# Low digits of x by ScalarE and an accumulating DMA, and causal masks of three units moved from TensorE to VectorE, in a fused attention and FFN kernel

## The chip, the cores and the metric

The kernel runs on one core of one Trainium2 chip. The metric is the device time of one execution in microseconds. Three runs of the kernel before gave 1025.21, 1024.13 and 1023.95 us, median 1024.13. The profiled execution took 1023.99 us.

A core has five engines, each with its own queue: TensorE (PE in the profile; its weight loads are PEld), VectorE (DVE), ScalarE (ACT), GpSimd (POOL) and SyncE (SP, which here only issues transfers). Each runs its own instructions in order and waits on semaphores of the others. Transfers (DMA) run beside them, issued here from SP's, ScalarE's and POOL's queues.

## The reference

One transformer block over x of 4 sequences x 512 positions x 1024 channels, in fp32:

```
q, k, v = x @ wq.T, x @ wk.T, x @ wv.T        # 16 heads of 64
q, k    = rope(q), rope(k)                    # pairs (x1, x2) -> (-x2, x1)
scores  = where(causal, q @ k.T, -1e9) / 8
a       = softmax(scores) @ v
x       = layernorm(x + a @ wo.T)
x       = layernorm(x + x @ (w8 * scales).T)  # w8 is int8
```

## The kernel before

**Digits.** A matmul with fp32 operands costs more on TensorE than one with the rounded type fp32r. So each fp32 operand is split: h is the operand times LESS = 1 - 2^-13, rounded to fp32r; l = x - h is the rest; d = h - l / X12 with X12 = 2^-12. A product is 16 matmuls of h with h and l with l, interleaved (the A part), and 8 of d with d (the D part), over 8 blocks of 128 channels; the two parts are combined with factors 1 + X12 and -X12. For x, h comes from ScalarE (`high_x`, L169), l from VectorE (`low_x`, L173), d from VectorE (`diff_x`, L177). Each of these instructions handles one of four chunks n of 2 x 512 columns per partition (512 KB in fp32). Weights are split likewise (L214, L215, L219, L223).

**Units.** There are 32 units, each a sequence b and a pair of heads: units 0 to 15 alternate between b = 0 and 1, units 16 to 31 between b = 2 and 3. The digits of two sequences are kept at a time: `XD[0]` for even b and `XD[1]` for odd. So around units 14 to 17 the digits of b = 2 and 3 replace those of 0 and 1. Near the end "b = 4" and "b = 5" stand for the two halves of the output weights wo, which take the places of the digits of x in the same way. `new_sequence` (L324) writes down when that is done, `load_x2` (L165) loads a chunk into one of three staging buffers (pool `stage`, which also holds staged weights, tiles of ao and rows of x).

**One unit's loop.** TensorE computes the scores of unit u (L409), and in between, as 72 "tickets", the products q, k, v of the coming units: (u+1, k), (u+1, v), (u+2, q). VectorE takes the maxima (L430), ScalarE the exponentials (L444), VectorE the reciprocals (L452), POOL the scaling (L458), VectorE the 32 x 32 transposes (L463); SP takes the probabilities through DRAM (`turned`, L464, then `prT`, L472) to finish the transposition. The values of a unit are turned in the same manner (`turn_values`: L464, then four transfers `va`, L482). TensorE then multiplies probabilities by values (`attend`, L490); ScalarE copies the result out (`ot`, L498) and issues its transfer to ao in DRAM (L499). The A part of a product is taken from PSUM by ScalarE (`tA`, L295), the D part by VectorE, which adds tA (L318). A and D tiles share a pool of two PSUM buffers (`pj`). For q and k SP swaps neighbouring rows (`rot<-raw`, two transfers, L249), and VectorE does the three rope steps (L235, L236, L242).

**Causal mask.** In the units listed in BUSY (L136) TensorE adds the mask to the diagonal blocks itself: eight matmuls of `unit` with `mask` in bfloat16 per unit (L419). In the other units VectorE adds it, four instructions per unit (L427).

**Order of work.** The order on TensorE, VectorE and ScalarE is that of the program text. Work for coming units is put into named slots of a loop with `later(u, slot, f)` and done there with `run(u, slot)`. The slots stand in this order: early, (maxima, exponentials of score groups 0 and 1), between, 18 tickets, (exponentials of group 2, attend u-1), after, first transposes, more tickets, first, turn, mid, tickets, second, tickets, late, tickets, values of u+1, tickets, end. The orders of SP and POOL are worked out by a scheduler from the dependences.

**The end.** Loops 30 and 31 also compute the first output products (`out_product`, L199) with the digits of wo; rows of x for the residual are loaded to the staging buffers or to the tables of cos and sin (`more_rows`, `rows_of_tables`), and VectorE adds the product to a row (L208). Then the int8 words of the FFN are loaded and cast (L620), and for each of 16 row tiles the output product, the norm, the transposition and the FFN product (`ffn`, L672) follow each other; POOL issues the transfers of the result (L685).

Of the kernel before, what the change touches and what calls it, by code (L numbers as in the profile page):

```python
# [38 lines left out]
def attention_ffn_kernel(  # L39
# [93 lines left out]
    units = [(b, hp) for hp in range(NHP) for b in (0, 1)] + [(b, hp) for hp in range(NHP)[::-1] for b in (2, 3)]  # L133
    NU = len(units)

    BUSY = (0, 1, NU // 2 - 2, NU // 2 - 1, NU - 2, NU - 1)  # L136
    qk, prod, va, plan = {}, {}, {}, {}


# [10 lines left out]
    def later(u, slot, f):  # L150
        plan.setdefault((u, slot), []).append(f)
# [19 lines left out]
    def low_x(b, n):  # L171
        h, l, d = (t[:, 2 * n : 2 * n + 2, :] for t in XD[b % 2])
        nc.vector.tensor_tensor(l, staged.pop((b, n)), h, SUB)  # L173

    def diff_x(b, n):
        h, l, d = (t[:, 2 * n : 2 * n + 2, :] for t in XD[b % 2])
# [52 lines left out]
    with tc.tile_pool(name="raw", bufs=2) as rawp, tc.tile_pool(name="qk", bufs=2) as qkp, ExitStack() as heads:  # L229
# [38 lines left out]
        def product(u, k, n):  # L268

            b, hp = units[u]  # L270
            w, r = WD[k], XD[b % 2]
            if n in (0, 2 * NC):
                prod["A" if n == 0 else "D"] = pjp.tile([P, S], FP, tag="pj", name=f"p_{u}_{k}_{n}")
            ps = prod["A" if n < 2 * NC else "D"]
            c, part = (n // 2, n % 2) if n < 2 * NC else (n - 2 * NC, 2)
            nc.tensor.matmul(  # L276
                ps,
                lhsT=w[part][:, c, :],
                rhs=r[part][:, c, :],
                start=n in (0, 2 * NC),  # L280
                stop=n in (2 * NC - 1, NT - 1),
            )
            last = u == NU - 1
            more = last or units[u + 1][1] != hp

            if more and n == 0:
                load_ao(k) if last else load_w(k, units[u + 1][1])

            b_next = units[u + 2][0] if u + 2 < NU else B + b % 2
            x_next = k == 2 and b_next != b  # L290
            if x_next and n == 0:
                new_sequence(u, b_next, True)
            if n == 2 * NC - 1:
                prod["tA"] = rawp.tile([P, S], FP, tag="tA", name=f"tA_{u}_{k}")
                nc.scalar.activation(prod["tA"], ps, AF.Copy, scale=1.0 + X12)  # L295
                if x_next:
                    new_sequence(u, b_next, False)
                if more:

                    scalar = ("after" if last else None, "first", None)[k]  # L300
                    if scalar:
                        later(u - 1, scalar, lambda: high_w(k))
                    else:
                        high_w(k)
                    vector = ((u - 1, "first"), (u - 1, "late"), (u, "between"))[k]
                    if u == 1:
                        vector = (None, vector, (1, "between"))[k]
                    if last and k != 1:
                        l, d = (((u - 1, "turn"), (u - 1, "mid")), None, ((u, "after"), (u, "after")))[k]
                        later(*l, lambda: low_w(k))  # L310
                        if k == 2:

                            later(*l, lambda: low_x(b_next, 0))
                        later(*d, lambda: diff_w(k))
                    else:
                        later(*vector, lambda: split_w(k))
            if n == NT - 1:
                nc.vector.scalar_tensor_tensor(raw_tile(u, k), ps, -X12, prod["tA"], op0=MUL, op1=ADD)  # L318
                if k < 2:
                    swap(u, k)  # L320
                    slot = ("first" if last else "between" if u % 2 else "late") if k == 0 else "turn"
                    later(u - 1, slot, lambda: rope(u, k))

        def new_sequence(u, b, begin):  # L324


            if b == B + 1:
                if begin:
                    later(u - 1, "mid", lambda: load_x2(b, 0))
            else:  # L330
                for n in range(3):
                    (load_x2 if begin else high_x)(b, n)
            if begin:
                return

            def each(f, *ns):
                return lambda: [f(b, n) for n in ns]

            if b <= B:
                steps = (  # L340
                    (u - 1, "late", each(low_x, 0)), (u - 1, "late", each(load_x2, 3)),
                    (u - 1, "late", each(low_x, 1, 2)), (u - 1, "end", each(high_x, 3)),
                    (u, "between", each(low_x, 3)), (u, "between", each(diff_x, 0, 1)),
                    (u, "late" if b == B else "first", each(diff_x, 2, 3)),
                )
            else:

                steps = (
                    (u - 1, "late", each(load_x2, 1)), (u - 1, "late", each(high_x, 0)),
                    (u - 1, "late", lambda: load_x2(b, 2, qkp.tile([P, 2, S], FP, tag="qk", name="last_2"))),  # L350
                    (u, "early", lambda: load_x2(b, 3, qkp.tile([P, 2, S], FP, tag="qk", name="last_3"))),
                    (u, "after", each(high_x, 1, 2)), (u, "first", lambda: more_rows(2)),
                    (u, "first", each(high_x, 3)), (u, "first", each(low_x, 1, 2)),
                    (u, "second", each(low_x, 3)), (u, "second", lambda: more_rows(3)),
                    (u, "late", each(diff_x, 0, 1, 2, 3)),
                )
            for step in steps:
                later(*step)

        def more_rows(t):  # L360
            row_tiles.append(stage(f"row_{t}", [P, E]))
            load_row(t)
# [140 lines left out]
        with tc.manual_schedule(  # L503
            engines={mybir.EngineType.PE, mybir.EngineType.DVE, mybir.EngineType.Activation}
        ):
            with tc.tile_pool(name="first", bufs=1) as firstp:
                raw_w = firstp.tile([P, 3, NC, P], FP, name="raw_w")
                raw_x0 = firstp.tile([P, NC, S], FP, name="raw_x")
                last_x1 = firstp.tile([P, 2, S], FP, name="last_x1")
                for c in range(0, NC, 2):  # L510
                    nc.sync.dma_start(out=raw_w[:, 0, c : c + 2, :], in_=wq[0, :, c : c + 2, :])
                    nc.scalar.dma_start(out=raw_x0[:, c, :], in_=xT[0, :, c, :])
                    nc.sync.dma_start(out=raw_x0[:, c + 1, :], in_=xT[0, :, c + 1, :])
                nc.sync.dma_start(out=raw_w[:, 1], in_=wk[0])
                load_x2(1, 0)
                nc.sync.dma_start(out=raw_w[:, 2], in_=wv[0])
                load_x2(1, 1)
                nc.sync.dma_start(out=cos_sb, in_=cos)
                nc.sync.dma_start(out=sin_sb, in_=sin)
                load_x2(1, 2)  # L520
                staged[1, 3] = last_x1
                nc.sync.dma_start(out=last_x1, in_=xT[1, :, 6:8, :])
                for n in range(NC // 2):
                    staged[0, n] = raw_x0[:, 2 * n : 2 * n + 2, :]
                raw_x = [[staged[b, n] for n in range(NC // 2)] for b in range(2)]


                def first_high_w(k):
                    nc.scalar.activation(WD[k][0], raw_w[:, k], AF.Copy, scale=LESS)

                def first_low_w(k):
                    nc.vector.tensor_tensor(raw_w[:, k], raw_w[:, k], WD[k][0], SUB)
                    nc.scalar.activation(WD[k][1], raw_w[:, k], AF.Copy, scale=1.0 / X12)

                for n in range(NC // 2):
                    high_x(0, n)
                    low_x(0, n)
                for n in range(3):
                    diff_x(0, n)
                whole_product(0, 0)  # L540
                first_high_w(1)
                for n in range(2):
                    high_x(1, n)
                    low_x(1, n)
                rope(0, 0)
                whole_product(0, 1)
                for n in range(2, 4):
                    high_x(1, n)
                    low_x(1, n)
                first_high_w(2)  # L550
                first_low_w(1)
                rope(0, 1)
                whole_product(0, 2)
                for n in range(2):
                    diff_x(1, n)
                first_low_w(2)
                for n in range(2, 4):
                    diff_x(1, n)
                diff_w(1)
                whole_product(1, 0)  # L560
                load_w(0, 1)
# [10 lines left out]
            for u in range(NU):  # L572
# [6 lines left out]
                run(u, "between")  # L579
                take(18)  # L580
                softmax(u, 2)
                if u:
                    attend(u - 1)
                run(u, "after")
# [183 lines left out]
```

## Time and profile before

| | |
|---|---|
| median of three runs | 1024.13 us |
| profiled execution | 1023.99 us |
| its span | 1022.2 us |
| TensorE busy | 1004.3 us, 98% |
| VectorE busy | 849.0 us, 83% |
| ScalarE busy | 388.9 us, 38% |
| POOL busy | 202.4 us, 20% |
| scores of unit 14 begin | 335.14 us |
| scores of unit 15 begin | 359.79 us |
| scores of unit 16 begin | 382.64 us |
| scores of a plain unit after the one before (77.85 to 99.30) | 21.45 us |

The span is from the first to the last instruction in the trace; the time of an execution is 1.8 us longer here. Matmuls overlap: 128x512 matmuls that follow each other without a pause start 0.227 us apart, although each lasts 0.39. The granted clock is that of TensorE, 1.00 when full. In a line of the timeline the columns are start, duration, engine, line of the kernel, operation, output and inputs, and in brackets the idle time of the engine before it with what ended it. In a line of the waits the columns are the waiting instruction, what it waited for, the total in us, how many times, and the longest. In a group's line the columns are the line, engine, operation and tiles, the count, the busy time in us and the mean of one in ns, and the idle time before. In a line of the transfers the columns are the tiles, the queue, the count, the size of one, and the median time in us from issue to landing.

### The profile page before, as it was taken

Reading aid. Unit: us, or ns where it says so; the run is one execution under the profiler, and the core shown is the slowest. Engines: PE = TensorE matmul, PEld = TensorE weight load, DVE = VectorE, ACT = ScalarE, POOL = GpSimd, SP = SyncE. Lnnn points to the kernel's source line nnn. Section 1 sums busy time; section 2 is a strip of 40 time slices with the busy share of each in tenths; the row PEclk is TensorE's granted clock in tenths of the full one; section 3 lists DMA queues with packets and bytes.
Section 4 is the critical chain, followed back from the end, with each engine's and each line's share of the span. In section 5 each row is a group of like instructions: output and inputs, shape, how many; then the busy total and the mean of one; then the engine's idle time right before and its main releaser. Section 6 shows DMA issues by size and latency. Waiting matters only on the chain.

```text
span 1022.2 us, 13786 instructions
## 1 busy us (share of the span) xinstructions
PE 1004.3 (98%) x4652; PEld 745.7 (73%) x4652; DVE 849.0 (83%) x1234; ACT 388.9 (38%) x841; POOL 202.4 (20%) x283
## 2 busy tenths in 40 slices
PE   9999999999999999999999999998899999999997
PEld 4667777777777677777777777776588888888885
DVE  5988888888888889888888888888898877878776
ACT  4524444354544434445344443444442122121110
POOL 0122232222322322332223322222200000000000
PEclk9999999999999999999999999999899999999998
DMA  7576676766768777676776768678645465553641
GB/s 287 168 232 218 203 230 189 264 214 212 216 201 265 240 250 235 188 247 199 246 219 202 236 195 257 216 239 272 221 130 156 126 160 139 133 166 103 144 104 62
DMA packets 264022, 204.09 MB, mean 200 GB/s; under 512 B 147600, under 2 KB 220304, under 8 KB 263824
## 3 DMA queue, kind: packets, MB, share of 16 engines
q1 hardware_dynamic: 256464, 185.64, 60.8%
q10 hardware_dynamic: 5328, 9.70, 2.6%
q0 software_dynamic: 2160, 7.87, 1.9%
q8 instruction: 37, 0.61, 0.2%
q14 instruction: 33, 0.27, 0.1%
HBM read 112.46 MB, written 73.92 MB: 182 GB/s over the span
## 4 chain that ended last, share of the span: by engine, by line
PE 86%; DMA 5%; DVE 5%; ACT 1%; issue 1%; SPq 0%; POOL 0%; DVEq 0%; ACTq 0%; POOLq 0%
PE p L276 43%; PE y L199 16%; PE f L672 11%; PE s L409 6%; PE o L490 6%; PE pw L261 2%; ACT pr L444 1%; DMA turned<-pr 1%; DMA sx<-in_wo 1%; DMA sx<-in_xT 1%; DVE pr L463 1%; DVE x_l L173 1%; DMA cos_sb<-in_x 1%; DMA raw_x<-in_xT 1%; POOL pr L458 0%
## 5 line engine op out<-in xcount | busy, mean ns | idle before, releaser
L458 POOL TENSOR_SCALAR pr<-pr,rden 128x128 f32<-128x128 f32 (+3 forms) x256 | 191.5, 770 | 531.3 <-DVE rden L452 369.0
L276 PE MATMUL p<-x_h,w_h 128*128 128x512 f32 x736 | 290.1, 394 | 0.0
L276 PE MATMUL p<-x_l,w_l 128*128 128x512 f32 x736 | 286.8, 390 | 0.0
L276 PE MATMUL p<-x_d,w_d 128*128 128x512 f32 x736 | 190.8, 395 | 1.2 <-DVE v L318 1.0
L276 PEld LDWEIGHTS p<-x_h,w_h 128*128 128x128 f32 x736 | 138.1, 188 | 48.1 <-issue 19.7
L444 ACT ACTIVATE pr<-s,nmx 128x128 f32<-128x128 f32 (+3 forms) x256 | 131.4, 530 | 100.0 <-DVE nmx L430 100.0
L276 PEld LDWEIGHTS p<-x_d,w_d 128*128 128x128 f32 x736 | 135.6, 188 | 34.1 <-issue 5.1
L276 PEld LDWEIGHTS p<-x_l,w_l 128*128 128x128 f32 x736 | 138.2, 188 | 28.1
L295 ACT ACTIVATE tA<-p 128x512 f32<-128x512 f32 x92 | 55.1, 599 | 219.8 <-PE p L276 219.7
L463 DVE STREAM_TRANSPOSE pr<-pr 128x768 f32<-128x768 f32 (+1 forms) x96 | 99.5, 1054 | 22.2 <-POOL pr L458 21.0
L199 PE MATMUL y<-x_h,w_h 128*128 128x512 f32 x256 | 102.9, 402 | 4.5 <-DVE row L208 3.8
L199 PE MATMUL y<-x_l,w_l 128*128 128x512 f32 x256 | 102.3, 400 | 1.9 <-DVE w_l L219 1.9
L430 DVE TENSOR_REDUCE nmx<-s 128x2 f32<-128x256 f32 (+3 forms) x128 | 101.3, 819 | 2.9 <-PE s L419 0.2
L672 PE MATMUL f<-wf,x1lo 128*128 128x512 f32 x240 | 93.5, 390 | 0.0
L672 PE MATMUL f<-wf,x1hi 128*128 128x512 f32 x240 | 93.5, 389 | 0.0
L409 PE MATMUL s<-qk 64*128 64x384 f32 (+3 forms) x512 | 82.6, 450 | 1.0 <-DVE qk L242 1.0
L490 PE MATMUL o<-prT,va 128*64 128x256 f32 (+3 forms) x512 | 76.0, 439 | 0.0
L223 DVE TENSOR_TENSOR w_d<-w_h,w_l 128x1024 fp32r<-128x1024 f32 x60 | 74.4, 1240 | 1.5
L318 DVE SCALAR_TENSOR_TENSOR raw<-p,tA 128x512 f32<-128x512 f32 x61 | 41.9, 687 | 38.2 <-PE p L276 38.1
L490 PEld LDWEIGHTS o<-prT,va 128*64 128x64 f32 x512 | 33.9, 136 | 45.6 <-issue 40.3
L199 PE MATMUL y<-x_d,w_d 128*128 128x512 f32 x256 | 63.7, 390 | 0.0
L199 PEld LDWEIGHTS y<-x_h,w_h 128*128 128x128 f32 x256 | 49.6, 194 | 16.0 <-DVE row L208 4.3
(112 smaller groups left out, 1157.0 us busy)
## 6 DMA issues: line engine op xcount, KB each, us to landing
turned<-pr SPq DMA_DIRECT2D x64, 384.0 KB, 3.3
rot<-raw SPq DMA_DIRECT2D x128, 128.0 KB, 2.4
turned<-pr SPq DMA_DIRECT2D x32, 512.0 KB, 4.5
prT<-turned SPq DMA_DIRECT2D x32, 512.0 KB, 5.0
prT<-turned SPq DMA_DIRECT2D x32, 384.0 KB, 4.2
turned_v<-v SPq DMA_DIRECT2D x32, 256.0 KB, 4.6
va<-turned_v SPq DMA_DIRECT2D x128, 64.0 KB, 2.6
prT<-turned SPq DMA_DIRECT2D x32, 256.0 KB, 3.3
```

The source lines that it names most:

```text
L199: nc.tensor.matmul(ps, lhsT=r[part][:, c, :], rhs=w[part][:, c, :], start=n in (0, 2 * NC), stop=n in (2 * NC - 1, NT - 1),)
L223: nc.vector.tensor_tensor(d, h, l, SUB)
L276: nc.tensor.matmul(ps, lhsT=w[part][:, c, :], rhs=r[part][:, c, :], start=n in (0, 2 * NC), stop=n in (2 * NC - 1, NT - 1),)
L295: nc.scalar.activation(prod["tA"], ps, AF.Copy, scale=1.0 + X12)
L318: nc.vector.scalar_tensor_tensor(raw_tile(u, k), ps, -X12, prod["tA"], op0=MUL, op1=ADD)
L409: nc.tensor.matmul(ps[:, j, at : at + n], lhsT=t[rows, 0, ts(i, P)], rhs=keys[rows, :, : (i + 1) * Q], start=True, stop=u not in BUSY,)
L430: nc.vector.tensor_reduce(nmx[:, 2 * i : 2 * i + 2], ps[:, :, at : at + n], AX.X, ALU.max, negate=True)
L444: nc.scalar.activation(pr[:, :, at // P : at // P + i + 1, j, :], ps[:, j, at : at + n].rearrange("p (r k s) -> p r k s", r=R, s=Q), AF.Ex ...
L458: nc.gpsimd.tensor_scalar(p, p, rden[:, m : m + 1], 1.0, ALU.mult, ALU.mult)
L463: nc.vector.transpose(t, t)
L490: nc.tensor.matmul(ps[j * D : (j + 1) * D, kb * P :], lhsT=v[:, kb, 2 * j : 2 * j + 2, :].rearrange("p a s -> p (a s)"), rhs=t[:, :, 4 * k ...
L672: nc.tensor.matmul(ps, lhsT=part[:, c, :], rhs=wfv[:, c, o], start=(c == 0 and part is hi), stop=(c == NC - 1 and part is lo),)
```

## The change

- BUSY holds three units instead of six: 0, 30 and 31. Units 1, 14 and 15 lose their mask matmuls (24 in all), and VectorE adds the mask there (12 instructions in all).
- A new `digits_x` makes h and l of a chunk. ScalarE makes h as before, then writes -LESS times the staged chunk, rounded to fp32r, into l; this is -h. Then a transfer from POOL's queue adds the staged chunk onto l in SBUF. It replaces the pair of ScalarE's h and VectorE's l for every chunk but the four of b = 0: 20 of 24.
- The places change. For b = 2, 3 and 4, chunks 0 to 2 are done where only h was made before (in the product (u, v), after the A part); the load of chunk 3 moves from slot late to slot end of loop u-1, and its digits to slot between of loop u. For b = 5, chunk 0 is done in (30, late), chunks 1 and 2 in a new slot "then" (after the exponentials of group 2), chunk 3 in slot first; the loads of two rows of x move to slot second. At the start the digits of b = 1 are made in the same places by the new function.

The diff:

```diff
-    BUSY = (0, 1, NU // 2 - 2, NU // 2 - 1, NU - 2, NU - 1)
+    BUSY = (0, NU - 2, NU - 1)
...
+    def digits_x(b, n):
+
+        h, l, d = (t[:, 2 * n : 2 * n + 2, :] for t in XD[b % 2])
+        high_x(b, n)
+        nc.scalar.activation(l, staged[b, n], AF.Copy, scale=-LESS)
+        nc.gpsimd.dma_start(out=l.bitcast(FP), in_=staged.pop((b, n)), accum_op=ADD)
...
                         later(*l, lambda: low_w(k))
-                        if k == 2:
-
-                            later(*l, lambda: low_x(b_next, 0))
                         later(*d, lambda: diff_w(k))
...
                 for n in range(3):
-                    (load_x2 if begin else high_x)(b, n)
+                    (load_x2 if begin else digits_x)(b, n)
...
             if b <= B:
                 steps = (
-                    (u - 1, "late", each(low_x, 0)), (u - 1, "late", each(load_x2, 3)),
-                    (u - 1, "late", each(low_x, 1, 2)), (u - 1, "end", each(high_x, 3)),
-                    (u, "between", each(low_x, 3)), (u, "between", each(diff_x, 0, 1)),
+                    (u - 1, "end", each(load_x2, 3)), (u, "between", each(digits_x, 3)),
+                    (u, "between", each(diff_x, 0, 1)),
                     (u, "late" if b == B else "first", each(diff_x, 2, 3)),
                 )
             else:
 
                 steps = (
-                    (u - 1, "late", each(load_x2, 1)), (u - 1, "late", each(high_x, 0)),
+                    (u - 1, "late", each(load_x2, 1)), (u - 1, "late", each(digits_x, 0)),
                     (u - 1, "late", lambda: load_x2(b, 2, qkp.tile([P, 2, S], FP, tag="qk", name="last_2"))),
                     (u, "early", lambda: load_x2(b, 3, qkp.tile([P, 2, S], FP, tag="qk", name="last_3"))),
-                    (u, "after", each(high_x, 1, 2)), (u, "first", lambda: more_rows(2)),
-                    (u, "first", each(high_x, 3)), (u, "first", each(low_x, 1, 2)),
-                    (u, "second", each(low_x, 3)), (u, "second", lambda: more_rows(3)),
+                    (u, "then", each(digits_x, 1, 2)), (u, "first", each(digits_x, 3)),
+                    (u, "second", lambda: (more_rows(2), more_rows(3))),
                     (u, "late", each(diff_x, 0, 1, 2, 3)),
                 )
...
                 for n in range(2):
-                    high_x(1, n)
-                    low_x(1, n)
+                    digits_x(1, n)
                 rope(0, 0)
                 whole_product(0, 1)
                 for n in range(2, 4):
-                    high_x(1, n)
-                    low_x(1, n)
+                    digits_x(1, n)
...
                 softmax(u, 2)
+                run(u, "then")
                 if u:
                     attend(u - 1)
```

## The prediction

> **What bounds the kernel now.** I read the page's busy shares first, then TensorE's waits, then the places of the longest waits in its timeline, then the granted clock there.
>
> ```profile
> PE 1004.3 (98%) x4652; PEld 745.7 (73%) x4652; DVE 849.0 (83%) x1234; ACT 388.9 (38%) x841; POOL 202.4 (20%) x283
> PE 86%; DMA 5%; DVE 5%; ACT 1%; issue 1%; SPq 0%; POOL 0%; DVEq 0%; ACTq 0%; POOLq 0%
> ```
>
> TensorE is busy 98% of the span and carries 86% of the chain that ended last. Time can only come from matmuls taken off TensorE, from its waits, or from its clock. VectorE has 17% free over the whole span. All of TensorE's waits:
>
> ```profile
> PE y L199 <- DVE row L208: 3.8, 1, 3.8
> PE y L199 <- DVE w_l L219: 1.9, 1, 1.9
> PE s L409 <- DVE qk L242: 1.0, 1, 1.0
> PE p L276 <- DVE v L318: 1.0, 1, 1.0
> PE y L199 <- DVE cos_sb L208: 0.6, 1, 0.6
> PE p L276 <- DVE raw L318: 0.2, 1, 0.2
> ```
>
> Apart from 1.5 us at the first memset and 0.2 for a load, TensorE waits 8.7 us in all, always for VectorE, in six places. The timeline shows where (the bracket is the idle time before):
>
> ```profile
> 350.94 2.11 PE L276 MATMUL p<-x_d,w_d 128*128 128x512 f32 x8 [0.21 <-DVE raw L318]
> 357.72 2.14 PE L276 MATMUL p<-x_d,w_d 128*128 128x512 f32 x8 [1.03 <-DVE v L318]
> 702.38 0.50 PE L199 MATMUL y<-x_l,w_l 128*128 128x512 f32 x1 [1.93 <-DVE w_l L219]
> 731.83 0.80 PE L199 MATMUL y<-x_h,w_h 128*128 128x512 f32 x1 [3.85 <-DVE row L208]
> ```
>
> Two lie in the loop of unit 14, where the digits change from batches 0 and 1 to 2 and 3; the others lie at the start (55.01, 1.04) and in loops 30 and 31. The windows view (columns: stretch, length, busy time of PE, PEld, DVE, ACT, POOL, granted clock, DMA share, GB/s) gives the clock:
>
> ```profile
> 350.90:359.80 8.90, 7.83 (x34) 5.86 (x34) 8.87 (x10) 3.90 (x5) 0.00 (x1) 1.00 0.83 265
> 703.00:706.40 3.40, 3.40 (x10) 2.63 (x9) 3.37 (x5) 0.00 (x0) 0.00 (x0) 0.50 1.02 357
> 730.30:737.10 6.80, 5.27 (x12) 4.14 (x13) 6.70 (x7) 0.00 (x0) 0.00 (x0) 0.50 0.91 273
> ```
>
> After the wait of 1.03 the clock stayed full. After 1.93 came 3.40 us at half, in which 10 matmuls ran at about 0.43 us each instead of 0.227; that costs 1.7. So a wait of some 2 us is charged almost twice.
>
> **The change part by part.** VectorE loses 20 subtractions and gains 12 mask additions; ScalarE gains 20 copies, POOL 20 transfers:
>
> ```profile
> L173 DVE TENSOR_TENSOR x_l<-sx,x_h 128x1024 fp32r<-128x1024 f32 x17 | 20.4, 1232 | 0.0
> L427 DVE TENSOR_TENSOR s<-s,mask 128x256 f32<-128x256 f32 x104 | 44.5, 427 | 3.6
> L169 ACT ACTIVATE x_h<-sx 128x1024 fp32r<-128x1024 f32 x17 | 17.3, 1054 | 25.1 <-DMA sx<-in_wo 13.0 <-DMA sx<-in_xT 11.7 <-ACT ot L498 0.4
> ```
>
> VectorE: 20 x 1.22 - 12 x 0.43 = 19.3 us less. ScalarE: 20 x 1.05 = 21 us more. Neither sum counts by itself; what counts is six places on TensorE. Against them stands that the low digit is now ready only when a transfer has landed, and that the staging buffer, of which there are three, is free only then. No row shows an accumulating transfer. The nearest:
>
> ```profile
> out<-row POOLq DMA_DIRECT2D x7, 512.0 KB, 4.0
> row<-in_x SPq DMA_DIRECT2D x8, 512.0 KB, 3.7
> sx<-in_xT SPq DMA_DIRECT2D x11, 512.0 KB, 5.5
> turned_v<-v SPq DMA_DIRECT2D x32, 256.0 KB, 4.6
> ```
>
> I bound the time L from issue to landing by 3.7 (the quickest 512 KB) and 9 (the table load at the start, 9.0), and take 5: POOL's own row of 4.0, raised because 512 KB takes 5.5 in the attention part.
>
> The Trainium skill, "DMA: Bandwidth & Descriptors", section "Anatomy of one DMA — SWDGE (gpsimd) path", fits 2.0 us plus bytes over 436 GB/s, an estimate of 3.2 us for 512 KB. POOL's row of 4.0 is longer already; by the page the forecast would be nearer to the faster rival.
>
> *Start.* Unit 1's eight mask matmuls leave TensorE. Scores with masks last 55.01 to 58.71, 3.70; those of a plain unit 77.85 to 80.21, 2.36. That is -1.34. The wait of 1.04 before them stays: VectorE's chain there hangs on unit 0's last exponentials, which stand on ScalarE behind the copy tA that TensorE releases (41.31). The low digits of batch 1 issue near 25 and are wanted near 38 by VectorE's queue, so 9 us is hidden. Bounds -2.4 (the wait goes too) and 0 (four additions, 1.7 us, delay unit 1's softmax as much). Taken: -1.34.
>
> *Loop of unit 14.* Masks -1.34; the two waits, 1.24, could go. The D product of (16,0) would then start at 357.72 - 1.34 - 1.24 = 355.1. But it needs the buffer that the evacuation of v_15 empties, behind rope (15,1) on VectorE. On SP the load of chunk 2 of batch 3 waits until the accumulation of chunk 3 of batch 2 has landed, and the turned probabilities and the swap of raw (15,1) are queued behind it. POOL issues that accumulation between the scalings of groups 1 and 2, near 346.0. Then: + L + 0.5 (load issue) + 0.5 (turned issue) + 0.6 (first half of the swap) + 2.4 (landing) + 2.05 (three rope steps) + 0.65 (evacuation) = 352.7 + L = 357.7. TensorE waits 2.6, and D starts as before: net 0.0. The clock: 2.6 is nearer to 1.93 than to 1.03, so +1.7. Taken: +1.7. Bounds: L = 3.7 gives 356.4, a wait of 1.3, no drop: -1.3; L = 9 gives 361.7: +4.0 + 1.7 = +5.7.
>
> *Loop of unit 15.* Masks -1.34. The load of chunk 3 of batch 3 was issued at 358.83, before the values were turned; now it stands on SP behind turned_v of unit 15 and its four va loads:
>
> ```profile
> 358.83 0.34 SPq L165 DMA_DIRECT2D sx<-in_xT  x1
> 361.72 0.33 SPq L464 DMA_DIRECT2D turned_v<-v  x1
> 365.04 2.58 SPq L482 DMA_DIRECT2D va<-turned_v  x4
> ```
>
> Count from E, the end of v_15's evacuation. Turned_v issues at E+0.8, lands at +5.4 (4.6), the va issues end at +8.0, a swap is between them, the load issues at +8.6, lands at +13.0 (4.4 as now), then h and l on ScalarE (2 x 1.05) and the copy tA of (16,1) (0.6): +15.7. TensorE wants that PSUM buffer for A of (16,2) at E+12.2, by the present timeline without masks. Wait 3.5, then 3.4 us at half clock, +1.7: -1.34 + 3.5 + 1.7 = +3.9. Bounds: turned_v landing in 3.3, as in this very unit, and the load in 3.7 give a wait of 1.5, below 1.93, no drop: +0.2; a load of 5.5 gives +5.0.
>
> The Trainium skill, "TensorE: Matmul & The Clock Gate", section "Why this matters for your kernels", asks for no idle gaps over about 3 us, since a whole idle window of 3.4 us halves the clock. The row at 702.38 speaks against it: 1.93 us was followed by a window at 0.50. By the rule the wait of 2.6 would keep the clock, and the sum would be 1.7 lower.
>
> *End.* Three low digits of wo's second half (1.18 + 2.34 us at 727.73) leave VectorE ahead of row L208, so the wait of 3.85 goes, and perhaps the half clock behind it (2.6). But the A product then needs digits whose transfers POOL issues after all scalings of unit 31 (717.82 + 7.08 = 724.9) and which land near 731; the differences (4.62) follow, and o of unit 31 starts at 736 at best instead of 739.99: -4.0. Not all reaches the end: the copy ot of unit 31 stands on ScalarE behind digits of a tile of ao that SP loads late (13.89 us of waiting at 738.54), and its transfer releases the int8 words, their casts and the first FFN product, which started without slack at 759.83. That caps the gain near 2. Behind the transfer of chunk 3 of wo's first half SP now holds a load of ao and the swap of raw (31,1): +0.7. Taken: -1.3. Bounds -4.2 and +2.5 (L = 9 makes that swap 4 later, less 1.5 of slack). The wait of 1.93 is for w_l and stays. POOL's 20 issues of 0.53 (its row for out) cost 10.6 us on an engine that is 80% idle: nothing, with the 80% as cover.
>
> Sum: -1.34 + 1.7 + 3.9 - 1.3 = +3.0 on the profiled execution's 1023.99, which is 0.14 below the median 1024.13: 1027.0.
>
> **The rivals.** *Faster.* Transfers land in 3.7 and the values in 3.3, no wait reaches 1.9, the clock stays: -1.34 - 1.3 + 0.2 - 3.0 = -5.4, about 1018.5. For it: POOL's 4.0, and the 3.3 seen in unit 15. Against it: the DMA engines are 0.75 and 0.81 busy in those two loops.
> *Same.* The new waits come, but without the half clock: 3.0 - 3.4 = -0.4, 1023.6.
> *Much slower.* L near 9, because three accumulations run together beside other transfers; it decides from L = 6.5, where unit 14's loop loses 1.5 more. All upper ends: -1.34 + 5.7 + 5.0 + 2.5 = +11.9, 1036.
> *It does not do what it says:* VectorE never was the limit, so only the 24 mask matmuls count: -4.0, 1020. TensorE's waits for it, 8.7 us, speak against.
>
> **How the numbers follow.** A measurement tells 0.2% (2.05 us) from no change: faster is below 1022.1, slower above 1026.2. Forecast 0.40 (1024.5 to 1030), faster rivals 0.28 together, same 0.18, much slower 0.14. A fifth of the forecast's own range lies below 1026.2: same 0.26, slower 0.46. The range 1018.0 to 1032.5 leaves out some 0.09 on either side.
>
> **What would show it.** In the changed profile: a wait of A of (16,2) for ScalarE's tA of about 3.5; a wait of D of (16,0) for v of about 2.6; clock 0.50 in windows between 355 and 380; the first A product of wo's second half no longer waiting for VectorE's row; the wait of 1.04 at unit 1 unchanged; landing of x_l from POOL's queue near 5. Wrong if the va loads do not hold back that load, or if ScalarE takes tA earlier.

## The result and the profile after

The changed kernel took 1054.62 us (median of 4 runs, 1053.96 to 1056.07), the kernel before beside it 1024.49; the ratio is 1.0303, 95% interval 1.0290 to 1.0316. It is slower by 3%, and outside the range of the prediction. The profiled execution has a span of 1053.0 us, 30.8 more than before.

Two lines of the page of the kernel after, busy times and the chain that ended last:

```profile
PE 1012.7 (96%) x4628; PEld 751.9 (71%) x4628; DVE 832.1 (79%) x1226; ACT 407.1 (39%) x861; POOL 215.2 (20%) x303
PE 83%; DMA 8%; DVE 5%; ACT 1%; issue 1%; SPq 1%; DVEq 0%; POOL 0%; ACTq 0%
```

VectorE did get lighter, by 16.9 us (19.3 forecast). But transfers now hold 8% of the chain, where it was 5%, and TensorE 83% in place of 86%. TensorE was given 24 matmuls less and yet is busy 8.4 us longer, since it ran at half clock more often (the granted clock is in the windows below). All waits of TensorE of 1 us and more, in the view of the waits of the kernel after:

```profile
PE p L283 <- ACT tA L302: 12.0, 3, 4.9
PE y L206 <- DMA x_l<-sx: 3.8, 1, 3.8
PE y L206 <- DVE v L322: 3.5, 1, 3.5
PE p L283 <- DVE v L322: 3.3, 1, 3.3
PE y L206 <- DMA x_l<-last: 3.2, 2, 1.8
PE o L492 <- DMA prT<-turned: 2.1, 1, 2.1
PE warm L81 <- DVE sin_sb L79: 1.5, 1, 1.5
PE f L673 <- DVE x1lo L647: 1.1, 1, 1.1
PE s L411 <- DVE qk L249: 1.0, 1, 1.0
```

The waits of 3.85 for VectorE's row and of 1.93 for w_l are gone, as the change would have it. In their place are three waits for ScalarE's tA, two for the evacuation of v, three for low digits themselves and one for turned probabilities. Each of these nine ends, when followed back, at a transfer: ScalarE stands before tA because a load (`sx`) is late, the evacuation of v stands behind a swap that is late. The table compares the two kernels by stretches between the first scores of units (in us, from the timelines; the scores of unit 16 begin at 382.57 before, not 382.64):

| stretch | before | after | difference |
|---|---|---|---|
| start to scores of unit 1 | 55.01 | 54.88 | -0.13 |
| loop of unit 1 | 22.77 | 22.05 | -0.72 |
| units 2 to 13 | 257.36 | 257.36 | 0.00 |
| loop of unit 14 | 24.65 | 32.17 | +7.52 |
| loop of unit 15 | 22.78 | 31.10 | +8.32 |
| units 16 to 29 | 300.25 | 300.25 | 0.00 |
| loop of unit 30 | 26.61 | 35.84 | +9.23 |
| scores of unit 31 to the first FFN product | 50.24 | 55.44 | +5.20 |
| from there to the end | 262.53 | 263.91 | +1.38 |

All but 1.38 us of what was lost was lost where digits are made (the 1.38 go with waits of 0.77 and 1.07 for the digits of the first FFN product). The windows view over the four long stretches (length, busy times, granted clock, DMA share, GB/s), first the kernel before, then the kernel after:

```profile
335.14:359.79 24.65, 23.41 (x114) 15.88 (x113) 21.88 (x28) 10.26 (x24) 8.06 (x8) 1.00 0.75 240
359.79:382.57 22.78, 22.78 (x114) 16.04 (x113) 20.35 (x28) 8.60 (x23) 7.08 (x8) 1.00 0.82 257
682.82:709.43 26.61, 24.68 (x113) 17.10 (x112) 23.02 (x31) 13.79 (x27) 7.09 (x8) 0.94 0.84 259
709.43:759.67 50.24, 45.75 (x210) 33.22 (x209) 42.74 (x57) 20.75 (x37) 8.31 (x9) 0.93 0.63 207
```

```profile
334.29:366.46 32.17, 25.24 (x105) 17.72 (x104) 19.01 (x28) 13.95 (x28) 10.04 (x13) 0.88 0.98 252
366.46:397.56 31.10, 25.58 (x106) 18.55 (x105) 18.84 (x28) 9.42 (x24) 7.14 (x9) 0.85 0.87 260
697.81:733.65 35.84, 27.44 (x113) 18.35 (x112) 20.30 (x27) 16.00 (x29) 8.18 (x11) 0.86 0.93 266
733.65:789.09 55.44, 47.61 (x209) 33.82 (x208) 37.58 (x50) 22.30 (x38) 9.64 (x12) 0.87 0.76 215
```

The DMA engines are 0.98 busy in the loop of unit 14 instead of 0.75, and move hardly more bytes per second (252 GB/s, 240 before). The clock falls to 0.85 to 0.88. In the loop of unit 14, TensorE waits 3.66 and 3.27, 6.9 us, and the clock of 0.88 is worth 0.12 x 32.17 = 3.9; less the masks (1.34) and the old waits (1.24) that makes 8.2, near the 7.5 seen. An estimate, since clock and waits are added as if they were apart.

### The profile page after: what moved, and what is told of

Its sections match the earlier page's. It is cut to its first block, busy times and chain, and to the rows that moved or that the text cites. A ratio compares the mean times of both kernels' runs of the same rounds, so it can differ in the third digit from the quotient of the medians.

```text
span 1053.0 us, 13822 instructions
## 1 busy us (share of the span) xinstructions
PE 1012.7 (96%) x4628; PEld 751.9 (71%) x4628; DVE 832.1 (79%) x1226; ACT 407.1 (39%) x861; POOL 215.2 (20%) x303
## 4 chain that ended last, share of the span: by engine, by line
PE 83%; DMA 8%; DVE 5%; ACT 1%; issue 1%; SPq 1%; DVEq 0%; POOL 0%; ACTq 0%
PE p L283 44%; PE y L206 13%; PE f L673 11%; PE s L411 6%; PE o L492 6%; DMA turned_v<-v 3%; PE pw L268 3%; DMA turned<-pr 2%; DMA rot<-raw 1%; DVE pr L465 1%; DMA cos_sb<-in_x 1%; DMA sc<-in_scales 0%; DMA raw_ao<-ao 0%; SPq L484 0%; DVE nmx L432 0%
## 5 line engine op out<-in xcount | busy, mean ns | idle before, releaser
L283 PE MATMUL p<-x_h,w_h 128*128 128x512 f32 x736 | 294.9, 401 | 12.0 <-ACT tA L302 12.0
L283 PE MATMUL p<-x_l,w_l 128*128 128x512 f32 x736 | 290.6, 395 | 0.0
L460 POOL TENSOR_SCALAR pr<-pr,rden 128x128 f32<-128x128 f32 (+3 forms) x256 | 187.0, 749 | 472.3 <-DVE rden L454 321.9
L283 PEld LDWEIGHTS p<-x_h,w_h 128*128 128x128 f32 x736 | 140.7, 191 | 64.5 <-issue 22.0
L283 PEld LDWEIGHTS p<-x_l,w_l 128*128 128x128 f32 x736 | 140.7, 191 | 28.9
L206 PE MATMUL y<-x_d,w_d 128*128 128x512 f32 x256 | 66.5, 403 | 3.5 <-DVE v L322 3.5
L242 DVE TENSOR_TENSOR rot<-rot,sin_sb 128x512 f32<-128x512 f32 x64 | 44.1, 688 | 30.7 <-DMA rot<-raw 30.7
```

Of the source, the lines that this page charges most:

```text
L206: nc.tensor.matmul(ps, lhsT=r[part][:, c, :], rhs=w[part][:, c, :], start=n in (0, 2 * NC), stop=n in (2 * NC - 1, NT - 1),)
L242: nc.vector.tensor_mul(rot, rot, sin_sb[:, k, :])
L283: nc.tensor.matmul(ps, lhsT=w[part][:, c, :], rhs=r[part][:, c, :], start=n in (0, 2 * NC), stop=n in (2 * NC - 1, NT - 1),)
L460: nc.gpsimd.tensor_scalar(p, p, rden[:, m : m + 1], 1.0, ALU.mult, ALU.mult)
```

## The experiments

Two theories were set against each other. **A**: the transfers cost; an adding transfer from SBUF to SBUF is dear for the DMA engines, lands late, and makes others late. **B**: the places cost; the load of chunk 3 now stands behind the turned values on SP, and its digits stand ahead of tA on ScalarE.

**VectorE adds instead of the transfer** (the change without its transfer: all new places, loads, masks and ScalarE copies).

```diff
-        nc.gpsimd.dma_start(out=l.bitcast(FP), in_=staged.pop((b, n)), accum_op=ADD)
...
+    def add_x(b, n):    # called in the slots where low_x stood before
+        l = XD[b % 2][1][:, 2 * n : 2 * n + 2, :]
+        nc.vector.tensor_tensor(l, l.bitcast(FP), staged.pop((b, n)), ADD)
```

> The changed kernel with its loads and ScalarE copies in the new places, but the staged chunk is added onto minus h by VectorE, in the slots where the kernel before subtracted, and no transfer is made for it. If the transfers are what costs (theory A), 1022 to 1030 us: only the later load of the third chunk is left. If the later places cost (theory B: the load of chunk 3 behind the turned values on SP, ScalarE's copies ahead of tA), 1045 us or more.

Measured: 1023.87 us, ratio 0.9997 (0.9987 to 1.0006). No difference from before can be told, though loop 15 took 25.45 us there, 2.7 more than before, and others a little less. Theory B falls as the cause of the 30 us, and so does the thought that ScalarE's 20 copies cost them, since this run has them too.

**The transfer in the old places** (the kernel before, and only the subtraction exchanged).

```diff
         nc.scalar.activation(h, staged[b, n], AF.Copy, scale=LESS)
+        if b:
+            nc.scalar.activation(XD[b % 2][1][:, 2 * n : 2 * n + 2, :], staged[b, n], AF.Copy, scale=-LESS)
...
-        nc.vector.tensor_tensor(l, staged.pop((b, n)), h, SUB)
+        if b:
+            nc.gpsimd.dma_start(out=l.bitcast(FP), in_=staged.pop((b, n)), accum_op=ADD)
+        else:
+            nc.vector.tensor_tensor(l, staged.pop((b, n)), h, SUB)
```

> The kernel before with its masks and its slots, but minus h from ScalarE behind each h, and the accumulating transfer issued in the slot where VectorE subtracted, for 20 of 24 chunks. Theory A (transfers are slow and slow the others): 1040 us or more, with 512 KB landing in 7 us or more and loops 14, 15 and 30 longer by some 5 to 10 us each. Theory B (places): within 1020 to 1030 us.

Measured: 1055.0 us, ratio 1.0296 (1.0280 to 1.0311), the same loss as the whole change; loops 14, 15 and 30 took 31.3, 31.9 and 34.5 us. The waits are others: TensorE's longest there are two for exponentials (5.8 and 7.1) and one that ended with a load of weights (7.3). With the run above this settles which part of the change did it: the transfer, in either set of places.

**A plain copy in place of the addition.**

```diff
-        nc.gpsimd.dma_start(out=l.bitcast(FP), in_=staged.pop((b, n)), accum_op=ADD)
+        nc.gpsimd.dma_start(out=l.bitcast(FP), in_=staged.pop((b, n)))
```

> The changed kernel with the transfer as a plain copy: the staged chunk overwrites l instead of being added, so the low digit is x instead of x - h. Same bytes moved, same places, same waits. If it is the adding that makes the transfer slow, it lands in 4 to 5 us as POOL's other 512 KB and the time falls to 1030 to 1038 us; if any 512 KB from SBUF to SBUF is as slow, 7.5 us to landing and 1050 us or more; theory B also expects 1050 or more, but with a landing of 4 to 5.

Measured: 1036.62 us, ratio 1.0126 (1.0101 to 1.0151). So 18 of the 30 us are the price of adding instead of copying; the landing, 5.6, is a little above the 4 to 5 expected. The transfers of the low digits, first in the kernel after, then with the plain copy (tiles, queue, count, KB each, median us to landing):

```profile
x_l<-sx POOLq DMA_DIRECT2D x17, 512.0 KB, 7.5
x_l<-last POOLq DMA_DIRECT2D x2, 512.0 KB, 12.5
x_l<-last_x POOLq DMA_DIRECT2D x1, 512.0 KB, 7.8
```

```profile
x_l<-sx POOLq DMA_DIRECT2D x17, 512.0 KB, 5.6
x_l<-last POOLq DMA_DIRECT2D x2, 512.0 KB, 7.9
x_l<-last_x POOLq DMA_DIRECT2D x1, 512.0 KB, 2.9
```

The third line is one and the same transfer, issued near 24.6 us in both: 2.9 us to copy, 7.8 to add. Part of the 7.8 is queueing, since the adding transfer before it, issued at 22.68, landed only at 29.8. A cleaner pair, with none close before it, is chunk 3 of batch 3: 4.6 us to add (issued at 383.67), 2.9 to copy (issued at 376.36). The load on the engines is in the row of POOL's queue (packets, MB, share of the 16 engines' span), of the kernel before, the kernel after and the plain copy in this order:

```profile
q0 software_dynamic: 2160, 7.87, 1.9%
```

```profile
q0 software_dynamic: 5040, 18.35, 7.2%
```

```profile
q0 software_dynamic: 5040, 18.35, 4.6%
```

Same packets, same bytes. 7.2% of 1053.0 less 1.9% of 1022.2 is 56.4 us of all 16 engines for 20 transfers, 2.8 us each; with copying it is 28.2 us, 1.4 each. Adding took twice the engines' time. That is no effect of crowding: in the traces' packet records a packet of 4096 bytes of these transfers takes 0.33 us with adding and 0.16 with copying (medians), near the start as in loops 14 and 15. The copy at the start lands in 2.9, and the Trainium skill, "DMA: Bandwidth & Descriptors", section "Anatomy of one DMA — SWDGE (gpsimd) path", gives an estimate of 3.2 us by its fit; this run agrees with it for copying. For adding the measurement, 4.6 at the least, differs and decides.

**An eighth of the bytes.**

```diff
-        nc.gpsimd.dma_start(out=l.bitcast(FP), in_=staged.pop((b, n)), accum_op=ADD)
+        nc.gpsimd.dma_start(out=l.bitcast(FP)[:, :, :64], in_=staged.pop((b, n))[:, :, :64], accum_op=ADD)
```

> The changed kernel with the adding transfer cut to an eighth of its columns (64 of 512 in each block); in the rest of l minus h is left standing. Same places, same number of transfers, an eighth of the bytes. Theory A in the form that the bytes load the DMA engines: transfers land in 2 to 3 us, 1023 to 1031 us. If a fixed cost of each transfer or the places set the time: above 1042 us.

Measured: 1039.57 us, ratio 1.0151 (1.0135 to 1.0168), between the two expectations, and landings well above the 2 to 3 us expected:

```profile
x_l<-sx POOLq DMA_DIRECT2D x17, 64.0 KB, 5.2
x_l<-last POOLq DMA_DIRECT2D x2, 64.0 KB, 4.7
x_l<-last_x POOLq DMA_DIRECT2D x1, 64.0 KB, 2.8
```

Bytes carry half of the loss; the other half stays with an eighth of them. An eighth of the bytes is not an eighth of the load either. The row of POOL's queue in this run has more packets, not fewer:

```profile
q0 software_dynamic: 7600, 9.18, 3.4%
```

By the same sum as above that is 0.8 us of the 16 engines for each transfer, where 512 KB took 2.8. SP's queue in the loop of unit 14 of this run shows what else costs:

```profile
340.87 9.79 SPq L165 DMA_DIRECT2D sx<-in_xT  x3
350.75 0.38 SPq L466 DMA_DIRECT2D turned<-pr  x1
351.22 1.14 SPq L256 DMA_DIRECT2D rot<-raw  x2
```

The last of the three loads waits until a staging buffer is free, that is until the transfer of chunk 3 of batch 2 has landed, at 350.3 (POOL issued it at 346.53, behind its scalings). The turned probabilities and the swap of raw (15,1) are queued behind it, rope and the evacuation of v behind these, and TensorE waits 5.3 us for v. This is the chain of the prediction.

**The staging buffer freed early** (full bytes, then an eighth; the transfer of b = 2 and 3 reads a table that stays in SBUF).

```diff
-        nc.gpsimd.dma_start(out=l.bitcast(FP), in_=staged.pop((b, n)), accum_op=ADD)
+        t = staged.pop((b, n))
+        nc.gpsimd.dma_start(out=l.bitcast(FP), in_=cos_sb if b in (2, 3) else t, accum_op=ADD)
```

> The changed kernel, but for b = 2 and 3 the transfer adds the cos table onto l instead of the staged chunk (the low digit is then cos - h, rounded): same bytes, same adding, same landing that TensorE and VectorE wait for, but the staging buffer is free as soon as ScalarE has read it. Theory A1 (the buffer held until the transfer lands, and SP's queue behind the load that waits for it, is what costs): the loops of units 14 and 15 fall from 32.2 and 31.1 us to below 27 each, 1041 to 1046 us. Theory A2 (the adding transfers load the DMA engines and make every other transfer late): they stay above 29 each, 1049 to 1056 us.

> The adding transfer cut to an eighth of its columns, and for b = 2 and 3 taken from the cos table, so that the staging buffers of those chunks are free once ScalarE has read them; in the rest of l minus h is left standing. Both parts of the cost are then small in the loops of units 14 and 15. If load of the DMA engines and the held buffer are all there is, these loops return to 24.7 and 23 us, as with VectorE's addition (24.74 and 25.45), while loop 30 and the end stay as with an eighth alone: 1031 to 1036 us. If the places (the load of chunk 3 late, its digits ahead of tA on ScalarE) cost by themselves, the two loops stay at 28.5 and 26: 1037 us or more.

Measured: with full bytes 1052.71 us, ratio 1.0288 (1.0270 to 1.0306), loops 29.95 and 28.87: the first is just above and the second just under the bound of 29, so most of the cost stays (A2) and some of it goes (A1). With an eighth 1028.78 us, ratio 1.0048 (1.0031 to 1.0064), loops 25.34 and 21.81; the total is lower than expected, since loop 30 took 27.5 us against 29.2 with an eighth alone, and loops 16 to 29 and the stretch to the first FFN product about 1 us less each. What is left against the kernel before, 3.2 us of the span, lies in loop 30 and behind it. The four runs make a table of loops 14 and 15 together (47.43 us before, 47.40 with the masks alone moved; one profile each):

| | buffer held until landing | buffer free after ScalarE |
|---|---|---|
| 512 KB added | 63.27 | 58.82 |
| 64 KB added | 55.05 | 47.15 |

Either remedy alone leaves 7.6 or 11.4 us of the 15.8 lost; both together leave nothing. So in these loops the loss is the load of the adding transfers on the DMA engines and the buffer that they hold, and as the table reads, the two strengthen each other: the slower the landing, the longer SP stands. With both remedies the new places cost nothing there, nor do POOL's issues. For loop 30 and the end the freed buffer was not tried; an eighth of the bytes alone brought loop 30 from 35.8 to 29.2 us (26.6 before).

**Chunk 3's digits later on ScalarE.**

```diff
-                    (u - 1, "end", each(load_x2, 3)), (u, "between", each(digits_x, 3)),
+                    (u - 1, "end", each(load_x2, 3)), (u, "after", each(digits_x, 3)),
```

> The changed kernel with one place changed: for b = 2, 3 and 4 the digits of chunk 3 stand in slot after instead of between, so that ScalarE's copy tA and the exponentials of group 2 no longer stand behind a load that is late. In the profile after, three waits for tA took 12.0 us and drew half clock behind them. If that place is the cost, 1036 to 1044 us. If the transfers are late anyway and the work is only held up elsewhere (the evacuation of v, the turned probabilities), 1048 to 1058 us.

Measured: 1054.68 us, ratio 1.0308 (1.0290 to 1.0327): no change. The waits for tA fell from 12.0 to 6.6 us (one of 5.2, one of 1.4), and the time came back as waits for raw (3.0), for a row's half in cos_sb (1.9) and for the digits x1hi of the first FFN product (3.5 instead of 0.8); those for v and for low digits stayed, 5.8 and 6.5 against 6.8 and 7.0. That ScalarE stands before tA is where the lateness shows, not where it comes from.

**The masks alone**, and three attempts at something better. The first puts BUSY to 0, 30 and 31 in the kernel before; the second has VectorE's subtraction throughout, the mask of unit 1 alone moved, and the new places for wo alone; the third adds to the second that POOL subtracts the last three chunks of wo; a fourth lets POOL subtract everywhere in the kernel before. The new places for wo in the second and third follow the diff of the change, and are left out here.

```diff
-    BUSY = (0, 1, NU // 2 - 2, NU // 2 - 1, NU - 2, NU - 1)
+    BUSY = (0, NU - 2, NU - 1)                              # masks alone
+    BUSY = (0, NU // 2 - 2, NU // 2 - 1, NU - 2, NU - 1)    # mixed
...
-        nc.vector.tensor_tensor(l, staged.pop((b, n)), h, SUB)
+        (nc.gpsimd if b else nc.vector).tensor_tensor(l, staged.pop((b, n)), h, SUB)              # POOL everywhere
+        (nc.gpsimd if b > B and n else nc.vector).tensor_tensor(l, staged.pop((b, n)), h, SUB)    # mixed, POOL last
```

> The kernel before with only the masks of units 1, 14 and 15 moved to VectorE. Unit 1's loop gave 0.72 us back in the changed kernel, and should here. In the loops of units 14 and 15 VectorE is the one waited for and gets 1.7 us more in each, so the 1.34 us that each loses on TensorE may come back as waits: between -3.4 (all gains kept) and +3 (a new wait with a half clock), 1020.7 to 1027 us. More than 1028 would say that the masks have a part in the 30 us.

> A version meant to beat both: the kernel before with VectorE's subtraction throughout, unit 1's mask on VectorE, and the new places for the two halves of wo alone. The run with VectorE's addition showed the loop of unit 1 0.4, that of unit 30 1.2 and the stretch to the first FFN product 0.9 us shorter than before, while unit 15's was 2.7 longer, which is left as before here: 1021.0 to 1022.5 us. 1024 or more would say that these gains hang on the other places.

> The kernel before with masks, slots and loads as they were, and the subtraction of 20 of 24 low digits done by POOL instead of VectorE: no transfer, and VectorE is relieved as the change wanted. If relieving VectorE is worth what it waits for, 1014 to 1022 us; if POOL's subtraction of 128x1024 takes more than 3 us, or stands behind its scalings, TensorE waits for it instead: 1024 to 1035 us.

> The mixed version with one thing more: the low digits of chunks 1 to 3 of the second half of wo are subtracted by POOL (2.8 us each) once it has done unit 31's scalings, instead of by VectorE. With POOL subtracting everywhere the stretch from the scores of unit 31 to the first FFN product was 46.72 us against 50.24 before: 1018 to 1021.5 us. 1023 or more would say that the shorter stretch came from the other relief of VectorE.

Measured: masks alone 1022.94 us, ratio 0.9993 (0.9984 to 1.0003); mixed 1023.19, 0.9992 (0.9983 to 1.0000); POOL everywhere 1036.52, 1.0118 (1.0105 to 1.0131); mixed with POOL last 1027.39, 1.0031 (1.0021 to 1.0042; no trace of it is read). The masks have no part in the 30 us, and bring nothing in loop 15 (22.81 us against 22.78) and loop 14, where TensorE's waits for VectorE grew as much as the masks had taken:

```profile
350.20 2.11 PE L276 MATMUL p<-x_d,w_d 128*128 128x512 f32 x8 [1.47 <-DVE raw L318]
357.00 2.12 PE L276 MATMUL p<-x_d,w_d 128*128 128x512 f32 x8 [1.06 <-DVE v L318]
```

That is 2.53 with the masks on VectorE against 1.24, and a loop of 24.59 against 24.65. Masks alone and the mixed version are the quickest of the study, but both intervals reach 1: a gain is not shown. POOL everywhere came out just above its second range: POOL's subtraction took 2.35 to 3.36 us a chunk, against VectorE's 1.22, and qk came late for three scores, 9.8 us in all. The end with POOL everywhere was short, 46.72 us, but with POOL in the last chunks alone the whole was 4 us longer than the mixed version. By its expectation the short end then came from VectorE's other relief; what took the 4 us back is open.

## Why the prediction was wrong

**The sign leaned right, the size was a tenth.** Forecast +3.0, measured +30.8 in the profile. The chance of slower was 0.46, and the rival at 1036 had the right cause, late transfers, with 0.14. But its sum of all upper ends, with L = 9, is +11.9: a larger L alone does not make the 30.8.

**The term L held for one transfer and not for three in a row.** It was taken as 5, bounded by 3.7 and 9. The transfer that the sum of the loop of unit 14 prices, chunk 3 of batch 2, landed after 5.8 (issued at 348.35). Chunks 0 to 2 are issued 1.9 us apart, from 329.94 on, and landed after 5.9, 9.6 and 12.0, each behind the one before. The middle of the 17 is 7.5, that of the last chunks 12.5 and the longest 13.1, beyond the bound. The prediction took the price of a copy for an addition, and no row of before could show it.

**The step that failed: the DMA engines' time was put at nothing.** The step that costed POOL's 20 issues at nothing counted the issuing engine and not the 16 engines that carry the bytes. Before, these were 0.75 and 0.82 busy in the loops of units 14 and 15, which leaves 6.2 and 4.1 us, 10.3 together (an estimate that takes a share of 1.00 as full). The eight transfers of batches 2 and 3, issued from 329.9 to 383.7, in these loops or just ahead of them, need 8 x 2.8 = 22.6 us, and do not fit. Share times length of the two loops did grow by 21.4 us, from 37.2 to 58.6. Eight copies would need 11.3, and nearly fit. So what stood behind them came late. The load of chunk 3 of batch 2, issued at 335.87, let ScalarE start only at 346.05, 10.2 us later, just when the third of the adding transfers ahead of it had landed (345.7); loads of this kind took 4.2 to 6.2 us there before. The swap of raw (15,1), 2.4 in the sum, took 4.1 and 4.3. It now stands right behind a load on SP, and was as late with copies (5.0 and 5.8) and with an eighth (5.0 and 4.7), so the adding alone is not its reason.

**The chain in the loop of unit 14 had the right order.** D of (16,0) waited for v, 3.27 against 2.6 forecast. Its start, 357.7 by the sum, came at 362.75: POOL issued the transfer 2.35 us later (348.35 against 346.0), it landed 0.8 later, the swap 1.7 later. Ahead of it lay a wait of 3.66 for tA, which the sum did not have: the late load of chunk 3 again. It delayed TensorE too, so that 3.27 is so near to 2.6 is in part luck.

```profile
348.59 0.79 PE L283 MATMUL p<-x_h,w_h 128*128 128x512 f32 x1 [3.66 <-ACT tA L302]
362.75 3.78 PE L283 MATMUL p<-x_d,w_d 128*128 128x512 f32 x8 [3.27 <-DVE v L322]
376.48 2.37 PE L492 MATMUL o<-prT,va 128*64 128x512 f32 x16 [2.07 <-DMA prT<-turned]
383.91 0.80 PE L283 MATMUL p<-x_h,w_h 128*128 128x512 f32 x1 [3.45 <-ACT tA L302]
714.66 0.80 PE L283 MATMUL p<-x_h,w_h 128*128 128x512 f32 x1 [4.89 <-ACT tA L302]
730.23 3.49 PE L206 MATMUL y<-x_d,w_d 128*128 128x512 f32 x8 [3.51 <-DVE v L322]
756.20 0.79 PE L206 MATMUL y<-x_l,w_l 128*128 128x512 f32 x1 [3.82 <-DMA x_l<-sx]
```

**The loop of unit 15** had its wait for tA in the order forecast, but that 3.45 meets 3.5 is luck. The turned values took 9.6 us to land instead of 4.6, so the load was issued 14.1 us after the evacuation of v_15 ended (362.69), not 8.6, and tA was done after 21.2, not 15.7; TensorE, held up as well, wanted the buffer after 17.8, not 12.2. Two errors of 5.5 us cancelled. The run with late digits shows that the place was not the cause: moved away, the time came back elsewhere. A wait of 2.07 for turned probabilities came on top. The half clock was mis-sized as well: 3.4 us of it were charged behind a wait of 3.5, and it lasted 6.83 us behind 3.45 and behind 3.27 (of the latter 2.44 us fall into this loop), as the row of before at 730.30 already shows, 6.80 us behind 3.85. (In the prediction's row at 703.00 eight matmuls start, 0.427 us apart, not ten; 8 x 0.2 = 1.6, so the charge of 1.7 stands.) The windows of the kernel after, in the columns of before:

```profile
362.07:368.90 6.83, 6.15 (x20) 4.43 (x22) 2.73 (x6) 0.00 (x0) 0.00 (x0) 0.50 1.08 215
376.40:382.50 6.10, 3.98 (x22) 2.31 (x22) 0.00 (x0) 1.13 (x2) 1.73 (x4) 1.00 0.92 284
382.55:389.38 6.83, 5.47 (x13) 4.31 (x14) 4.15 (x6) 3.12 (x7) 2.24 (x3) 0.50 0.70 188
```

Waits of 2.07 and 3.45, 4.6 for 9.27 us at half clock, less 1.34 for the masks make +8.8, near the +8.32 seen; the forecast was +3.9.

**Loop 30 was priced at 0.7 and cost 9.23.** The same two waits as in loop 14 were there to be counted, 4.89 and 3.51, each with half clock behind it. The step looked at one swap behind one transfer, not at the chain that it had worked out for unit 14.

**At the end** the wait for the row went, as forecast, but the low digits landed 9 to 13 us after their issue (747.3 to 750.4), at 756 to 764. Counted from the first scores of unit 31 (733.65) that is 22.5 to 30 us, where the forecast had 21.6 (731 against 709.43). TensorE waited for three of them, 7.1 us in all, and half clock followed: +5.2 instead of -1.3.

**The start** was right in sign: the mask of unit 1 gave 0.72 of the 1.34, here and with the masks alone, and the wait of 1.04 stayed. The rival that only the masks would count, 1020, fell with the run of the masks alone, 1022.94 and not to be told from before.

## What to carry to other kernels

A transfer that computes is not priced by a row of transfers that copy: here the same 512 KB took the DMA engines twice as long, and landed after 4.6 us instead of 2.9 with none of its kind just before it, and after up to 13 in a row. Before work is moved to DMA, put its engine time beside what the DMA engines have free in that very stretch, and ask what the source buffer holds back until it lands and what is queued behind that on the issuing queue. If one chain is found in one stage, price it in every stage where the same code runs.

## What had not been expected of the hardware

The length of a wait alone did not tell whether the clock fell. Waits of 1.73 us (masks alone, 712.60), 1.93 (kernel before, 702.38) and 2.27 (an eighth, free buffer, 356.27) were each followed by 3.4 us at 0.50. Waits of 2.03 (VectorE adds, 351.19) and 2.07 (kernel after, 376.48) were followed by 3.40 and 6 us at 1.00. The Trainium skill, "TensorE: Matmul & The Clock Gate", section "What's actually happening", says that the window which decides is about 3.4 us long and runs free of the kernel. The length agrees: the half-clock stretches read here last 3.4 us or 6.8. None of these waits is a whole window long. That the same wait can fall differently into such windows fits the five rows. Counted back in steps of 3.413 us from a half-clock stretch of the same run, the three waits lie whole in one step, and the two are split over two steps (1.73 and 0.30, 1.31 and 0.76). That is a hint from five waits and was not tried on its own. A stretch can so move by 1 or 2 us with no edit in it: loop 30 took 26.61 us before, where w_l was waited for 1.93 us with half clock behind it, and 24.86 with the masks alone, where the wait was 0.64 and none followed. A difference of that size in one profile proves little.

An adding transfer of 64 KB in pieces of 256 bytes landed hardly sooner than a copying one of 512 KB (5.2 and 5.6 us in the middle, 2.8 and 2.9 for the transfer issued near 24.6). Why adding takes the engines twice as long was not tried.
